# Two graph-attention layers in their factored form, with leaky slope, mask and softmax written out, in place of a merged weight and of maxima of exponentials

## The chip, the core and the metric

The kernel runs on one core of a Trainium2 chip. The metric is the device time of one execution in microseconds (us); the kernel before was run three times and took 3838.46 us in the median (3838.01 to 3841.55). One of these executions was profiled.

A core has a matrix engine (PE, TensorE), a vector engine (DVE, VectorE), an activation engine (ACT, ScalarE), a general engine (POOL, GpSimd) and a queue that issues transfers (SP). They run side by side, each in the order of its own instructions, and wait for each other by semaphores.

## What is computed

64 sequences of 256 positions and 256 features, all in fp32, pass through two blocks. The first block holds two graph-attention layers, then a residual sum with layernorm and a Relu feed-forward with layernorm. The second is a relational attention of 8 heads, then layernorm, a Gelu feed-forward and layernorm. The change touches only the graph-attention layers:

```python
def _gat(h, adj, W, a, out_features):
    Wh = jnp.matmul(h, W)
    Wh1 = jnp.matmul(Wh, a[:out_features])
    Wh2 = jnp.matmul(Wh, a[out_features:])
    e = Wh1 + jnp.swapaxes(Wh2, 1, 2)
    e = jax.nn.leaky_relu(e, negative_slope=ALPHA)
    scores = jnp.where(adj > 0, e, NEG)
    att = jax.nn.softmax(scores, axis=1)
    return jnp.matmul(att, Wh)

h = _gat(x, adj, W1, a1, Fout)
h = _gat(h, adj, W2, a2, W2.shape[1])
h = _layernorm(x + h, g_ln1, b_ln1)
```

The softmax runs over the rows (axis 1) of each sequence, so with the transposed adjacency `adjT`, which the host lays out, it runs along the free axis of a tile.

## The kernel before

Two sequences make a pair, and there are 32 pairs. A tile of a pair holds its 512 rows as four blocks of 128 partitions (index `k`; sequence `b` is `k // 2`). Products are 128x128 weights against up to 512 columns; each writes into one of 8 PSUM banks that all the work shares (`bank()`).

Each pair passes through four generators: `gat_layers`, `then_ff` (layernorm, Relu feed-forward, layernorm), `attention`, and `then_out` (projection by Wo, layernorm, Gelu feed-forward, layernorm, store). `together` steps two generators in turn, one `yield` each. The main loop runs `attention(pair)` with `then_ff(pair + 1)`, and then `then_out(pair)` with `gat_layers(pair + 2)`. Before the loop, `gat_layers(0)` runs alone and `gat_layers(1)` beside `then_ff(0)`; so 30 of the 32 graph-attention stages run beside a `then_out`. A scheduler then orders each engine's instructions, near the order in which the steps are written.

What the two graph layers do before the change:

- Setup (L113 to L121): W1 times [W2, W2 a2, a1] is multiplied once into `w12`, of 260 columns. Four columns of it give the scores of both layers.
- L376: `y = x w12`, 260 columns per block, copied out by ACT (L378). It contains the values of both layers' weights and the two scores of layer 1.
- `gat_weights` (L158 to L180): instead of exp(leaky(e1 + e2)) it uses the larger of two products of exponentials. ACT makes `up`, `low` and `ratio` of four columns each (L162 to L164), PE spreads `up` and `low` along rows by transposes of broadcast columns (L151), ACT copies one of the two (L168). DVE then makes `e` by a multiply and maximum (L174), and masks it with a maximum and a minimum against `adjT`, with the row sums beside it (L176). The reciprocal of the sums scales the values (L178, L180).
- L387: `e` times the scaled values, 258 columns, copied out by ACT (L389). Two of the columns are the scores of layer 2, so there is no second product with a weight.
- `gat_weights` again, then L398: `e` times values, and the residual sum (L220).

`steep` records the largest score for a range test at the end of the kernel (L158, L444). If a test fails, a general routine, which the change doesn't touch, computes everything anew; its code isn't shown here.

Other lines that are spoken of: L206 and L207 are the transposes of rows ahead of a feed-forward or of the attention, L232 and L235 its first product and activation, L245 its second product, L359 the projection by Wo, L189 to L198 layernorm, L193 its power on POOL, L215 the addition of a bias on POOL, L327 to L331 the division after the attention, L307 the mask of relation 1, L369 the largest value of `adjT`.

Of the kernel before, what the change touches and what calls it, by code (L numbers as in the profile page):

```python
# [10 lines left out]
F32 = mybir.dt.float32  # L11
I32 = mybir.dt.int32
U8 = mybir.dt.uint8
U32 = mybir.dt.uint32
AF = mybir.ActivationFunctionType
ALU = mybir.AluOpType
AX = mybir.AxisListType

P = 128
NEG = -9000000000000000.0  # L20
ALPHA = 0.2
EPS = 1e-5
SAFE = 1e25
STEEP = 30.0
SHIFT = 40.0
EVEN = 1e-37


@with_exitstack
def two_layers(ctx: ExitStack, tc: tile.TileContext, t: dict, out: bass.AP, flag: bass.AP):  # L30

# [5 lines left out]
    nc = tc.nc  # L40
    B, N, D = out.shape
    NPAIR = B // 2
    KC = D // P
# [9 lines left out]
    const = ctx.enter_context(tc.tile_pool(name="const", bufs=1))  # L53
# [12 lines left out]
    loaded = {0: load(0)}  # L66


    ident = const.tile([P, P], F32, name="ident")
    make_identity(nc, ident)  # L70
    shift = const.tile([P, 1], F32, name="shift")
    nc.vector.memset(shift, -SHIFT)
    mhalf = const.tile([P, 4], F32, name="mhalf")
    nc.vector.memset(mhalf, -0.5)
    ones = const.tile([P, DH], F32, name="ones")
    nc.vector.memset(ones, 1.0)
    reach = const.tile([P, NPAIR, 2 * KC], F32, name="reach")
    most = const.tile([P, NPAIR, 4], F32, name="most")
    steep = const.tile([P, NPAIR, 2], F32, name="steep")

    def weights(name, pool=const):
        w = t[name]
        kc, m = w.shape[0] // P, w.shape[1]
        s = pool.tile([P, kc, m], F32, name="w_" + name)
        nc.sync.dma_start(s, w.rearrange("(c p) m -> p c m", p=P))
        return s

    def on_all(name, n, pool=const):

        v = t[name]  # L90
        s = pool.tile([P, n], F32, name="b_" + name)
        nc.sync.dma_start(s, bass.AP(tensor=v.tensor, offset=v.offset, ap=[[0, P], [1, n]]))
        return s

    def column(name):
# [2 lines left out]
        nc.sync.dma_start(s, t[name])  # L98
        return s

    w12 = const.tile([P, KC, D + 4], F32, name="w12")
    with tc.tile_pool(name="setup", bufs=1) as setup, \
            tc.tile_pool(name="psetup", bufs=2, space=bass.MemoryType.PSUM) as psetup:
        w1T, a2 = weights("L0_gnn_W1T", setup), on_all("L0_gnn_a2", 2 * D, setup)
        right = setup.tile([P, KC, D + 4], F32, name="right")
        nc.sync.dma_start(right[:, :, :D], t["L0_gnn_W2"].rearrange("(c p) m -> p c m", p=P))
        nc.sync.dma_start(right[:, :, D + 2:], t["L0_gnn_a1c"])
        junk = setup.tile([P, D], F32, name="junk")  # L110
        for s in range(2):
            for c in range(KC):
                nc.vector.scalar_tensor_tensor(  # L113
                    junk, right[:, c, :D], 1.0, a2[:, s * D:(s + 1) * D], op0=ALU.mult, op1=ALU.mult,
                    accum_out=right[:, c, D + s:D + s + 1])
        for m in range(KC):
            pw = psetup.tile([P, 512], F32, name="pw")
            for c in range(KC):
                nc.tensor.matmul(pw[:, :D + 4], lhsT=w1T[:, c, m * P:(m + 1) * P], rhs=right[:, c],
                                 start=c == 0, stop=c == KC - 1)  # L120
            nc.vector.tensor_copy(w12[:, m], pw[:, :D + 4])  # L121
    ln = [tuple(on_all(n, D) for n in names) for names in (
        ("L0_gnn_g_ln1", "L0_gnn_b_ln1"), ("L0_gnn_g_ln2", "L0_gnn_b_ln2"),
        ("L1_gnn_g1", "L1_gnn_beta1"), ("L1_gnn_g2", "L1_gnn_beta2"))]
# [13 lines left out]
    work = ctx.enter_context(tc.tile_pool(name="work", bufs=1))  # L138
# [3 lines left out]
    def bank():  # L142
        return psum.tile([P, 512], F32, name="ps")

    def on_rows(col):

        p = bank()
        for k in range(4):  # L150
            nc.tensor.transpose(p[:, k * P:(k + 1) * P], col[:, k:k + 1].to_broadcast([P, P]), ident)  # L151
        return p

    def gat_weights(y, at, layer, pair, empty):

        nc.vector.tensor_reduce(steep[:, pair, layer:layer + 1], y[:, :, at:at + 2], axis=AX.XY, op=ALU.max,  # L158
                                apply_absolute_value=True)
        e1, e2 = y[:, :, at], y[:, :, at + 1]  # L160
        up, low, ratio = (small.tile([P, 4], F32, name=n) for n in ("up", "low", "ratio"))
        nc.scalar.activation(up, e1, AF.Exp, bias=shift[:, 0:1])  # L162
        nc.scalar.activation(low, e1, AF.Exp, bias=shift[:, 0:1], scale=ALPHA)
        nc.scalar.activation(ratio, e2, AF.Exp, scale=ALPHA - 1.0)  # L164
        yield
        p_up, p_low = on_rows(up), on_rows(low)
        rows_up = work.tile([P, 512], F32, name="rows_up")
        nc.scalar.activation(rows_up, p_up, AF.Copy)  # L168
        e = work.tile([P, 4, N], F32, name="e", bufs=2)
        adjT = loaded[pair][1]  # L170
        sums, rs = small.tile([P, 4], F32, name="sums"), small.tile([P, 4], F32, name="rs")
        for k in range(4):
            s = slice(k // 2 * N, k // 2 * N + N)
            nc.vector.scalar_tensor_tensor(e[:, k], p_low[:, s], ratio[:, k:k + 1], rows_up[:, s],  # L174
                                           op0=ALU.mult, op1=ALU.max)
            nc.vector.scalar_tensor_tensor(e[:, k], adjT[:, k], empty[:, k:k + 1], e[:, k],  # L176
                                           op0=ALU.max, op1=ALU.min, accum_out=sums[:, k:k + 1])
        nc.vector.reciprocal(rs, sums)  # L178
        for k in range(4):
            nc.vector.tensor_scalar(y[:, k, :at], y[:, k, :at], rs[:, k:k + 1], None, ALU.mult)  # L180
        yield
        return e

    def layernorm(r, gb):
        g, b = gb
# [180 lines left out]

    def gat_layers(pair):
        xT, adjT, x = loaded[pair]
        nc.vector.tensor_reduce(most[:, pair], adjT.bitcast(U32), axis=AX.X, op=ALU.max)  # L369
        empty = small.tile([P, 4], F32, name="empty")  # L370
        nc.vector.tensor_scalar(empty, most[:, pair], 0.0, EVEN, ALU.is_le, ALU.mult)
        y = work.tile([P, 4, D + 4], F32, name="xw", bufs=2)
        for k in range(4):
            ps = bank()
            for c in range(KC):
                nc.tensor.matmul(ps[:, :D + 4], lhsT=xT[:, c, k * P:(k + 1) * P], rhs=w12[:, c],  # L376
                                 start=c == 0, stop=c == KC - 1)
            nc.scalar.activation(y[:, k], ps[:, :D + 4], AF.Copy)  # L378
        yield
        e = yield from gat_weights(y, D + 2, 0, pair, empty)  # L380
        z = work.tile([P, 4, D + 2], F32, name="axw", bufs=2)
        for b in range(2):
            for i in range(2):
                ps = bank()
                for j in range(2):
                    k = 2 * b + j
                    nc.tensor.matmul(ps[:, :D + 2], lhsT=e[:, k, i * P:(i + 1) * P], rhs=y[:, k, :D + 2],  # L387
                                     start=j == 0, stop=j == 1)
                nc.scalar.activation(z[:, 2 * b + i], ps[:, :D + 2], AF.Copy)  # L389
        yield  # L390
        e = yield from gat_weights(z, D, 1, pair, empty)
        r = rows_tile()
        for b in range(2):
            ps = bank()
            for i in range(2):
                for j in range(2):
                    k = 2 * b + j
                    nc.tensor.matmul(ps[:, i * D:(i + 1) * D], lhsT=e[:, k, i * P:(i + 1) * P], rhs=z[:, k, :D],  # L398
                                     start=j == 0, stop=j == 1)
            add_rows(r, ps, x, b)  # L400
        rows[pair] = r
# [35 lines left out]
        del loaded[pair]  # L437


    ranges = ((reach, NPAIR * 4, N * SAFE), (most, NPAIR * 4, 1.0), (steep, NPAIR * 2, STEEP))  # L440
    count = const.tile([P, len(ranges)], F32, name="count")
    for n, (found, width, most_allowed) in enumerate(ranges):
        kept = const.tile([P, width], F32, name=f"kept{n}")
        nc.vector.tensor_scalar(kept, found.rearrange("p a b -> p (a b)"), most_allowed, None, ALU.is_le,  # L444
                                ALU.add, accum_out=count[:, n:n + 1])
    total = bank()
    nc.tensor.matmul(total[:1, :len(ranges)], lhsT=ones[:, :1], rhs=count, start=True, stop=True)
    all_of_them = const.tile([1, 1], F32, name="all_of_them")
    nc.vector.tensor_reduce(all_of_them, total[:1, :len(ranges)], axis=AX.X, op=ALU.add)
    nc.vector.tensor_scalar(flag, all_of_them, P * sum(w for _, w, _ in ranges) - 0.5, None, ALU.is_lt)  # L450


@with_exitstack
# [421 lines left out]
```

## Time and profile before

| what | value |
|---|---|
| median of three runs | 3838.46 us |
| the profiled execution | 3841.55 us |
| its span, from first to last instruction | 3839.8 us |
| mean granted clock of TensorE | 0.964 of full |
| ACT table loads (L235, L298), each | 63, 1.283 us |
| L376, x16 a pair, busy | 124.4 us |
| L151, x16 a pair, busy | 78.7 us |
| L387, x16 a pair, busy | 193.8 us |
| L398, x16 a pair, busy | 119.8 us |
| L174 and L176 on DVE, busy | 111.2 and 137.3 us |

Busy times are sums over the span of the time in which an engine worked on that group of instructions, overlaps counted once. An engine's row in the strip of 40 slices gives its busy tenths, and PEclk the clock that TensorE was granted, also in tenths. A weight load (PEld) runs ahead of, and beside, the products.

### The profile page before, as it was taken

The page shows a single profiled execution, that of the slowest core. Times are in us where ns is not written, and L with a number is a line of the kernel's source. Part 1 is how long each engine was busy: PE and PEld are TensorE (multiplying, and loading weights), DVE is VectorE, ACT ScalarE, POOL GpSimd, SP SyncE. Part 2 cuts the span into 40 slices and gives each one's busy share as a digit, 9 for nine tenths or more (in the row PEclk, how much of TensorE's full clock was granted, in tenths as well). Part 3 has the DMA queues.
Part 4 walks back from the last instruction along what each step waited for, and adds up shares of the span by engine and source line. Part 5 has one row for each costly group of instructions (what it writes and reads, how often), then busy time and mean ns, then how long its engine had stood idle before and what let it go on. Part 6 is the DMA issues. An engine that isn't in the chain of part 4 may idle for free. (4 is left out here: it accounts for less than half of the span.)

```text
span 3839.8 us, 46320 instructions
## 1 busy us (share of the span) xinstructions
PE 3530.9 (92%) x18698; PEld 2201.9 (57%) x18698; DVE 1967.2 (51%) x4825; ACT 1055.5 (27%) x1920; POOL 443.8 (12%) x518
## 2 busy tenths in 40 slices
PE   6999999999999999999999999999999999999998
PEld 4565565555655556556556565565565655656555
DVE  4454545545555455455454554555545545545444
ACT  1223223233222232222322323223233222232222
POOL 0111101101101011011110111110101101111010
PEclk9999999999999999999999999999999999999999
DMA  4000000000000000000000000000000000000000
GB/s 133 12 17 22 17 17 17 23 17 17 22 17 17 17 17 23 17 17 17 17 22 17 17 23 17 17 19 16 22 17 17 22 17 17 17 17 22 1 6 13
DMA packets 66862, 78.16 MB, mean 20 GB/s; under 512 B 3281, under 2 KB 57681, under 8 KB 66641
## 3 DMA queue, kind: packets, MB, share of 16 engines
q1 hardware_dynamic: 66640, 75.13, 6.2%
q8 instruction: 149, 2.44, 0.3%
q14 instruction: 73, 0.59, 0.0%
HBM read 58.34 MB, written 16.78 MB: 20 GB/s over the span
## 5 line engine op out<-in xcount | busy, mean ns | idle before, releaser
L232 PE MATMUL ps<-yT,w_L_gnn_w_ff 128*128 128x512 f32 x1024 | 473.2, 605 | 0.1
L245 PE MATMUL ps<-w_L_gnn_w_ff,ff 128*128 128x256 f32 x2048 | 467.1, 384 | 0.0
L232 PE MATMUL ps<-yT,w_L_gnn_W 128*128 128x512 f32 x1024 | 459.5, 597 | 1.0 <-ACT yT L207 1.0
L245 PE MATMUL ps<-w_L_gnn_W,ff 128*128 128x256 f32 x2048 | 447.2, 379 | 0.0
L245 PEld LDWEIGHTS ps<-w_L_gnn_w_ff,ff 128*128 128x128 f32 x2048 | 381.4, 190 | 83.9 <-issue 35.8
L245 PEld LDWEIGHTS ps<-w_L_gnn_W,ff 128*128 128x128 f32 x2048 | 389.1, 190 | 66.6 <-issue 15.3
L220 DVE TENSOR_TENSOR y<-ps,y 128x512 f32<-128x512 f32 x192 | 130.8, 681 | 536.7 <-PE ps L245 534.4
L307 DVE TENSOR_TENSOR m<-a,adjT 128x512 f32<-128x512 f32 x512 | 316.8, 686 | 147.2 <-ACT a L298 147.2
L327 DVE RECIPROCAL s<-ps 128x256 f32<-128x256 f32 x128 | 224.2, 1752 | 236.8 <-PE ps L321 236.8
L193 POOL TENSOR_TENSOR rstd<-rstd,mhalf 128x4 f32<-128x4 f32 x128 | 142.0, 1109 | 1732.2 <-DVE rstd L192 1732.2
L298 ACT ACTIVATE a<-ps 128x512 f32<-128x512 f32 x512 | 261.0, 614 | 215.7 <-PE ps L293 215.6
L232 PEld LDWEIGHTS ps<-yT,w_L_gnn_w_ff 128*128 128x128 f32 x1024 | 184.1, 189 | 233.2 <-issue 192.2
L232 PEld LDWEIGHTS ps<-yT,w_L_gnn_W 128*128 128x128 f32 x1024 | 193.8, 192 | 209.0 <-issue 195.7
L387 PE MATMUL ps<-xw,e 128*128 128x258 f32 x512 | 193.8, 559 | 129.9 <-DVE xw L180 129.9
L235 ACT ACTIVATE ff<-ps,c_L_gnn_b_ff 128x512 f32<-128x512 f32 x256 | 176.5, 690 | 373.2 <-PE ps L232 373.2
L235 ACT ACTIVATE ff<-ps,c_L_gnn_b 128x512 f32<-128x512 f32 x256 | 176.0, 687 | 369.6 <-PE ps L232 369.2
L378 ACT ACTIVATE xw<-ps 128x260 f32<-128x260 f32 x128 | 49.6, 387 | 769.0 <-PE ps L376 769.0
L387 PEld LDWEIGHTS ps<-xw,e 128*128 128x128 f32 x512 | 146.8, 294 | 172.1 <-DVE xw L180 138.1
L215 POOL TENSOR_TENSOR y<-y,b_L_gnn_bo 128x256 f32<-128x256 f32 x128 | 94.6, 770 | 1304.2 <-PE ps L206 1304.2
L174 DVE SCALAR_TENSOR_TENSOR e<-ps,ratio,rows_up 128x256 f32<-128x256 f32 x256 | 111.2, 474 | 236.2 <-ACT rows_up L168 235.2
L258 PE MATMUL ps<-wv,yTa 128*128 128x512 f32 x512 | 230.3, 592 | 0.0
L189 DVE BATCH_NORM_STATS2 st<-y 128x6 f32<-128x256 f32 x512 | 194.4, 412 | 5.4
(89 smaller groups left out, 4098.0 us busy)
## 6 DMA issues: line engine op xcount, KB each, us to landing
xT<-in_xT SPq DMA_DIRECT2D x32, 512.0 KB, 3.7
adjT<-in_adjT SPq DMA_DIRECT2D x32, 512.0 KB, 4.0
x<-in_x SPq DMA_DIRECT2D x32, 512.0 KB, 4.0
out<-y SPq DMA_DIRECT2D x32, 512.0 KB, 2.9
w_L_gnn_w_ff<-in_L_gnn_w_ff SPq DMA_DIRECT2D x2, 1024.0 KB, 10.4
w_L_gnn_W<-in_L_gnn_W SPq DMA_DIRECT2D x2, 1024.0 KB, 7.2
wv<-in_L_gnn_Wv SPq DMA_DIRECT2D x2, 256.0 KB, 7.2
w_L_gnn_W1T<-in_L_gnn_W1T SPq DMA_DIRECT2D x1, 256.0 KB, 6.8
```

The source lines that it names most:

```text
L174: nc.vector.scalar_tensor_tensor(e[:, k], p_low[:, s], ratio[:, k:k + 1], rows_up[:, s], op0=ALU.mult, op1=ALU.max)
L189: nc.vector.bn_stats(st[:, k, :], r[:, k, :])
L193: nc.gpsimd.tensor_tensor(rstd, rstd, mhalf, ALU.pow)
L220: nc.vector.tensor_tensor(r[:, s, :].rearrange("p k d -> p (k d)"), p, y[:, s, :].rearrange("p k d -> p (k d)"), ALU.add)
L232: nc.tensor.matmul(p1, lhsT=w1[:, c, m * P:(m + 1) * P], rhs=yT[:, c, :], start=c == 0, stop=c == KC - 1)
L235: nc.scalar.activation(h, p1, func, bias=b1[:, m:m + 1])
L245: nc.tensor.matmul(p2[:, j * D:(j + 1) * D], lhsT=f[m][:, k * P:(k + 1) * P], rhs=w2[:, m, :], start=m == 0, stop=m == NF - 1)
L258: nc.tensor.matmul(ps, lhsT=yT[:, c, at:at + P], rhs=wv[:, c].rearrange("p r m -> p (r m)"), start=c == 0, stop=c == KC - 1)
L298: nc.scalar.activation(a, ps[o], AF.Exp)
L307: nc.vector.tensor_tensor(m, a, adj, ALU.mult)
L327: nc.vector.reciprocal(s, po[:, N:])
L387: nc.tensor.matmul(ps[:, :D + 2], lhsT=e[:, k, i * P:(i + 1) * P], rhs=y[:, k, :D + 2], start=j == 0, stop=j == 1)
```

## The change

The merged weight, the exponentials of the scores and the transposes go. Each layer now does what the reference writes. `p1` is the first score of all columns, spread on all partitions by a weight whose columns are all the same (`wide`); `p2` is the second score, one column per block. ACT adds them, DVE applies the leaky slope, writes NEG where `adjT` isn't positive and takes the row maximum, ACT takes Exp with row sums. The values are a product of their own, scaled by the reciprocal of the sums while they are copied from PSUM. Layer 1 writes its result transposed (`hT`), as layer 2 takes it. `masked` is made once per pair. The range test on `steep` goes. The products of the heads with the relations' values, in the second block, are the same in both kernels.

```diff
-    w12 = const.tile([P, KC, D + 4], F32, name="w12")
...
+    def gat_weights(w_name, a_name, setup):
+
+        w = weights(w_name)
+        a = on_all(a_name, 2 * D, setup)
+        wa = const.tile([P, 2, KC, 1], F32, name="wa_" + w_name)
+        junk = setup.tile([P, D], F32, name="junk")
+        for s in range(2):
+            for c in range(KC):
+                nc.vector.scalar_tensor_tensor(
+                    junk, w[:, c, :], 1.0, a[:, s * D:(s + 1) * D], op0=ALU.mult, op1=ALU.mult,
+                    accum_out=wa[:, s, c, :])
+        wide = const.tile([P, KC, P], F32, name="wide_" + w_name)
+        for c in range(KC):
+            nc.vector.tensor_copy(wide[:, c, :], wa[:, 0, c, :].to_broadcast([P, P]))
+        return w, wide, wa[:, 1]
...
-    def on_rows(col):
...
-    def gat_weights(y, at, layer, pair, empty):
...
+    def gat_attention(aT, gw, masked):
+
+        w, wide, wa2 = gw
+        p1 = bank()
+        for c in range(KC):
+            nc.tensor.matmul(p1, lhsT=wide[:, c, :], rhs=aT[:, c, :], start=c == 0, stop=c == KC - 1)
+        p2 = bank()
+        for k in range(4):
+            for c in range(KC):
+                nc.tensor.matmul(p2[:, k:k + 1], lhsT=aT[:, c, k * P:(k + 1) * P], rhs=wa2[:, c, :],
+                                 start=c == 0, stop=c == KC - 1)
+        wh2 = small.tile([P, 4], F32, name="wh2")
+        nc.vector.tensor_copy(wh2, p2[:, :4])
+        e = work.tile([P, 4, N], F32, name="e")
+        for k in range(4):
+            b = k // 2
+            nc.scalar.activation(e[:, k, :], p1[:, b * N:(b + 1) * N], AF.Identity, bias=wh2[:, k:k + 1])
+        yield
+        ef = e.rearrange("p k n -> p (k n)")
+        nc.vector.scalar_tensor_tensor(ef, ef, ALPHA, ef, op0=ALU.mult, op1=ALU.max)
+        nc.vector.copy_predicated(ef, masked, neg.to_broadcast([P, 4 * N]))
+        nm = small.tile([P, 4], F32, name="nm")
+        nc.vector.tensor_reduce(nm, e, axis=AX.X, op=ALU.max, negate=True)
+        sums = small.tile([P, 4], F32, name="sums")
+        for k in range(4):
+            nc.scalar.activation(e[:, k, :], e[:, k, :], AF.Exp, bias=nm[:, k:k + 1], accum_out=sums[:, k:k + 1])
+        yield
+        rs = small.tile([P, 4], F32, name="rs")
         nc.vector.reciprocal(rs, sums)
-        for k in range(4):
-            nc.vector.tensor_scalar(y[:, k, :at], y[:, k, :at], rs[:, k:k + 1], None, ALU.mult)
-        yield
-        return e
+        wh = work.tile([P, 4, D], F32, name="wh")
+        for b in range(2):
+            pw = bank()
+            for j in range(2):
+                k = 2 * b + j
+                for c in range(KC):
+                    nc.tensor.matmul(pw[:, j * D:(j + 1) * D], lhsT=aT[:, c, k * P:(k + 1) * P], rhs=w[:, c, :],
+                                     start=c == 0, stop=c == KC - 1)
+            for j in range(2):
+                k = 2 * b + j
+                nc.vector.tensor_scalar(wh[:, k, :], pw[:, j * D:(j + 1) * D], rs[:, k:k + 1], None, ALU.mult)
+        yield
+        return e, wh
...
     def gat_layers(pair):
         xT, adjT, x = loaded[pair]
+        masked = work.tile([P, 4 * N], U8, name="masked")
+        nc.vector.tensor_scalar(masked, adjT.rearrange("p k n -> p (k n)"), 0.0, None, ALU.is_le)
         nc.vector.tensor_reduce(most[:, pair], adjT.bitcast(U32), axis=AX.X, op=ALU.max)
...
+        e, wh = yield from gat_attention(xT, gat1, masked)
+        hT = work.tile([P, KC, 512], F32, name="hT")
+        for c in range(KC):
             ps = bank()
+            for b in range(2):
+                for j in range(2):
+                    k = 2 * b + j
+                    nc.tensor.matmul(ps[:, b * N:(b + 1) * N], lhsT=wh[:, k, c * P:(c + 1) * P], rhs=e[:, k, :],
+                                     start=j == 0, stop=j == 1)
+            nc.scalar.activation(hT[:, c, :], ps, AF.Copy)
+        yield
+        e, wh = yield from gat_attention(hT, gat2, masked)
         r = rows_tile()
         for b in range(2):
             ps = bank()
             for i in range(2):
                 for j in range(2):
                     k = 2 * b + j
-                    nc.tensor.matmul(ps[:, i * D:(i + 1) * D], lhsT=e[:, k, i * P:(i + 1) * P], rhs=z[:, k, :D],
+                    nc.tensor.matmul(ps[:, i * D:(i + 1) * D], lhsT=e[:, k, i * P:(i + 1) * P], rhs=wh[:, k, :],
                                      start=j == 0, stop=j == 1)
             add_rows(r, ps, x, b)
         rows[pair] = r
```

More of the change, by code (lines that the diff above doesn't have):

```diff
@@ L23 @@
 SAFE = 1e25
-STEEP = 30.0
-SHIFT = 40.0
-EVEN = 1e-37
 @with_exitstack
@@ L70, in two_layers @@
     make_identity(nc, ident)
-    shift = const.tile([P, 1], F32, name="shift")
-    nc.vector.memset(shift, -SHIFT)
+    neg = const.tile([P, 1], F32, name="neg")
+    nc.vector.memset(neg, NEG)
     mhalf = const.tile([P, 4], F32, name="mhalf")
@@ L78, in two_layers, with weights @@
     most = const.tile([P, NPAIR, 4], F32, name="most")
-    steep = const.tile([P, NPAIR, 2], F32, name="steep")
-    def weights(name, pool=const):
+    def weights(name):
         w = t[name]
         kc, m = w.shape[0] // P, w.shape[1]
-        s = pool.tile([P, kc, m], F32, name="w_" + name)
+        s = const.tile([P, kc, m], F32, name="w_" + name)
         nc.sync.dma_start(s, w.rearrange("(c p) m -> p c m", p=P))
@@ L99, in column @@
         return s
-    w12 = const.tile([P, KC, D + 4], F32, name="w12")
[L104 to L109, printed above, removed]
+    def gat_weights(w_name, a_name, setup):
+        w = weights(w_name)
+        a = on_all(a_name, 2 * D, setup)
+        wa = const.tile([P, 2, KC, 1], F32, name="wa_" + w_name)
         junk = setup.tile([P, D], F32, name="junk")
@@ L113, in two_layers @@
                 nc.vector.scalar_tensor_tensor(
[L114 to L121, printed above, removed]
+                    junk, w[:, c, :], 1.0, a[:, s * D:(s + 1) * D], op0=ALU.mult, op1=ALU.mult,
[4 more added lines that the diff above has]
+        return w, wide, wa[:, 1]
+    with tc.tile_pool(name="setup", bufs=1) as setup:
+        gat1 = gat_weights("L0_gnn_W1", "L0_gnn_a1", setup)
+        gat2 = gat_weights("L0_gnn_W2", "L0_gnn_a2", setup)
     ln = [tuple(on_all(n, D) for n in names) for names in (
@@ L143, in bank @@
         return psum.tile([P, 512], F32, name="ps")
-    def on_rows(col):
-        p = bank()
-        for k in range(4):
-            nc.tensor.transpose(p[:, k * P:(k + 1) * P], col[:, k:k + 1].to_broadcast([P, P]), ident)
-        return p
-    def gat_weights(y, at, layer, pair, empty):
[L158 to L164, printed above, removed]
-        yield
[L166 to L171, printed above, removed]
-        for k in range(4):
[L173 to L177, printed above, removed]
-        nc.vector.reciprocal(rs, sums)
-        for k in range(4):
-            nc.vector.tensor_scalar(y[:, k, :at], y[:, k, :at], rs[:, k:k + 1], None, ALU.mult)
@@ L368, in gat_layers @@
         xT, adjT, x = loaded[pair]
+        masked = work.tile([P, 4 * N], U8, name="masked")
+        nc.vector.tensor_scalar(masked, adjT.rearrange("p k n -> p (k n)"), 0.0, None, ALU.is_le)
         nc.vector.tensor_reduce(most[:, pair], adjT.bitcast(U32), axis=AX.X, op=ALU.max)
[L370 to L373, printed above, removed]
+        e, wh = yield from gat_attention(xT, gat1, masked)
+        hT = work.tile([P, KC, 512], F32, name="hT")
+        for c in range(KC):
             ps = bank()
[L375 to L378, printed above, removed]
-        yield
[L380 to L384, printed above, removed]
+            for b in range(2):
                 for j in range(2):
                     k = 2 * b + j
-                    nc.tensor.matmul(ps[:, :D + 2], lhsT=e[:, k, i * P:(i + 1) * P], rhs=y[:, k, :D + 2],
+                    nc.tensor.matmul(ps[:, b * N:(b + 1) * N], lhsT=wh[:, k, c * P:(c + 1) * P], rhs=e[:, k, :],
                                      start=j == 0, stop=j == 1)
-                nc.scalar.activation(z[:, 2 * b + i], ps[:, :D + 2], AF.Copy)
+            nc.scalar.activation(hT[:, c, :], ps, AF.Copy)
         yield
-        e = yield from gat_weights(z, D, 1, pair, empty)
+        e, wh = yield from gat_attention(hT, gat2, masked)
         r = rows_tile()
@@ L437, in two_layers @@
         del loaded[pair]
[L440 to L444, printed above, removed]
+    count = const.tile([P, 2], F32, name="count")
+    for n, (values_of, most_allowed) in enumerate(((reach, N * SAFE), (most, 1.0))):
+        kept = const.tile([P, NPAIR * 4], F32, name=f"kept{n}")
+        nc.vector.tensor_scalar(kept, values_of.rearrange("p a b -> p (a b)"), most_allowed, None, ALU.is_le,
                                 ALU.add, accum_out=count[:, n:n + 1])
     total = bank()
[L447 to L450, printed above, removed]
+    nc.tensor.matmul(total[:1, :2], lhsT=ones[:, :1], rhs=count, start=True, stop=True)
+    both = const.tile([1, 1], F32, name="both")
+    nc.vector.tensor_reduce(both, total[:1, :2], axis=AX.X, op=ALU.add)
+    nc.vector.tensor_scalar(flag, both, 2 * P * NPAIR * 4 - 0.5, None, ALU.is_lt)
 @with_exitstack
@@ L859 @@
     laid["xT"] = np.ascontiguousarray(x.reshape(B // 2, 2, N, D).transpose(0, 3, 1, 2))
-    laid["L0_gnn_W1T"] = np.ascontiguousarray(laid["L0_gnn_W1"].T)
-    laid["L0_gnn_a1c"] = np.ascontiguousarray(laid["L0_gnn_a1"].reshape(2, -1, P).transpose(2, 1, 0))
     laid["adjT"] = np.ascontiguousarray(adj.transpose(0, 2, 1))
```

## Prediction

> **What bounds the kernel now.** I read the page's busy times first, then the strips in 40 slices, the waits of TensorE, the groups by shape, and last the timeline of one period.
>
> ```profile
> span 3839.8 us, 46320 instructions
> PE 3530.9 (92%) x18698; PEld 2201.9 (57%) x18698; DVE 1967.2 (51%) x4825; ACT 1055.5 (27%) x1920; POOL 443.8 (12%) x518
> PE   6999999999999999999999999999999999999998
> PEclk9999999999999999999999999999999999999999
> ```
>
> TensorE is busy 92% from end to end and no other engine passes 51%. What is left is 309 us of idle PE and whatever the clock strip hides, which is below full in every slice. The waits say where:
>
> ```profile
> PE ps L387 <- DVE xw L180: 129.9, 32, 4.2
> PE ps L206 <- DVE y L198: 54.0, 65, 4.2
> PE ps L398 <- DVE axw L180: 34.1, 32, 4.3
> PE ps L359 <- DVE oT L331: 31.5, 32, 3.1
> PE ps L151 <- ACT up L162: 26.0, 32, 0.9
> ```
>
> Columns: total us, times, longest. Nearly all of it lies once per pair of sequences, around the first graph layer. The timeline of TensorE there (start, length, group, idle before it):
>
> ```profile
> 1817.25 2.42 PE L359 MATMUL ps<-w_L_gnn_Wo,oT 128*128 128x256 f32 x10
> 1819.51 2.36 PE L376 MATMUL ps<-w,xT 128*128 128x260 f32 x10
> 1822.77 1.56 PE L359 MATMUL ps<-w_L_gnn_Wo,oT 128*128 128x256 f32 x6 [0.90 <-DVE oT L331]
> 1824.17 1.48 PE L376 MATMUL ps<-w,xT 128*128 128x260 f32 x6
> 1826.46 0.65 PE L151 MATMUL ps<-ident,up 128*128 128x128 f32 x4 [0.81 <-ACT up L162]
> 1826.95 0.60 PE L151 MATMUL ps<-ident,low 128*128 128x128 f32 x4
> 1828.45 1.14 PE L206 MATMUL ps<-ident,y 128*128 128x128 f32 x6 [0.91 <-DVE y L198]
> 1830.02 0.44 PE L206 MATMUL ps<-ident,y 128*128 128x128 f32 x2 [0.43 <-DVE y L198]
> 1834.64 6.28 PE L387 MATMUL ps<-xw,e 128*128 128x258 f32 x16 [4.19 <-DVE xw L180]
> ```
>
> The reader should see two things. From the Wo product to the product with e, PE idles 7.2 us. And the 16 instructions that end the row take 6.28 us, where the same shape (L376, x10 from 1819.51 to 1821.87) runs at 0.226 us each, 3.6 us in all: the clock has dropped. Their weight loads have a median of 337 ns against 190 at L376. Over all 32, L387 is busy 193.8 us, so (193.8 - 32 x 3.55) / 32 = 2.5 us of slow clock per pair. The period, from this L359 to the one two pairs on (2054.70), is 118.7 us a pair.
>
> [...] a 4.19 us gap, then about 6 us slow. [...] the mask step L176 took 0.85 and 0.93 us beside GpSimd's bias adds and 0.47 without.
>
> **The change, part by part.** An fp32 product is two PE instructions, a transpose one. PE rates from the timeline: 0.43 us per instruction of 512 columns (16 from 1722.27 to 1729.13), 0.22 of 256, 0.11 per transpose.
> Removed per pair: L376 16 x 0.226 = 3.6; the 16 transposes of L151 1.76; L387 at full clock 3.5. Sum 8.9 us.
> Added: the row score p1, 4 instructions of 512 a layer, 2 x 1.74 = 3.5; the column score p2, 16 instructions of one column a layer; wh, 16 of 256 a layer, 2 x 3.5 = 7.0; hT, 16 of 256, 3.5. The last product stays. The trace has no one-column product with full weights. [...] from above, a load that hides under nothing, 0.19 (the LDWEIGHTS rows), and what the three-column product L447 lasts beyond its own load, 0.17 - 0.08: 0.28. I take 0.12 since loads run ahead of products here: 2 x 1.92 = 3.8. Sum 17.8 us. PE gains 8.9 us of work a pair, 285 us in all, if all of it were on the path.
>
> Not all is: the first layer lies in the stretch with 7.2 us idle. I lay out both stretches, with time 0 at the first Wo product, in the order in which the changed code puts each engine's instructions.
>
> *Stretch A, to the end of the first product with e.* Before: 17.39 to the start of L387, 3.5 of work, 2.5 slow: 23.4. After, PE: ten Wo instructions to 2.26, p1 to 4.0, p2 to 5.9, two of wh, then the other six Wo (oT is ready at 5.5, so the 0.90 wait goes), to 7.7, the rest of wh to 10.8. Then PE waits for VectorE. VectorE is in order: it is done with oT at 5.46, waits for p2 and copies wh2 (6.3); layernorm of the first half (two bn_stats 0.75, aggregates 0.30, two L195 0.86) to 8.1, residual add 0.63, leaky 1.2 (ScalarE has made e in 4 x 0.3 by 7.6), bn_stats and one aggregate 0.87, copy_predicated, two L195, aggregate and rstd 1.1, row maximum 1.22 (the row of L369, 1024 elements), four L198 2.1. Leaky over 1024 is scaled from L307 (512 in 0.62): 1.2. copy_predicated isn't in the trace; from below one pass of 1024 (1.1), from above two (2.3); I take 1.2. The sum puts the last L198 at 16.4. ScalarE's four Exp, about 0.4 each from L378, start after the maximum at 14.3 and end beside L198. rs 0.2; the first scaled wh at 16.7. Then hT, 3.5 of work. PE was idle from 10.8 to about 14.6 and had only eight transposes until 16.7, so I let it pay the same 2.5 slow: end at 22.7. **Stretch A: -0.7 us.**
>
> *Stretch B, from there to the second feed-forward product.* Before 19.26 (1722.27 to 1741.53): L232 13.8, L151 0.88, L398 3.53, a wait of 0.96. After: L232 13.8, p1 1.74, p2 1.92, wh 3.5, the last product 3.53: 24.5. Do waits hide in it? ScalarE must do two more table loads a pair (Gelu, Exp, Gelu; 1.28 each in this trace). Counted from hT's end: e 7.4 to 9.0 after p2; maximum at 12.6; table load and Exp after the fifth Gelu, 13.1 to 16.2; wh scaled by 17.9; the last product is due at 21. That leaves 3 us, so the slower ScalarE costs nothing unless the chain slips by that; then each us beyond it is 30 us. Banks: the sixth Gelu frees its bank at 18.2, before the rotation needs it. **Stretch B: +5.2 us.**
>
> The rest of the period, 76 us, is untouched: most stays, and masked (1.2 us on VectorE) stands where VectorE waits for Exp. Loads of xT are released a few us later but are needed a whole stage later, and a load of 512 KB lands in 4 us.
>
> *Ends.* Pair 0 runs alone. The merged weight's setup on PE (12.04 to 16.4) goes, but each layer now has leaky, mask, maximum, Exp and wh in a row; I add them up to about 49 us against 46.2 at the end of its last product: +3. Pair 1 beside a Relu feed-forward: 8.9 of work less about 2 of waits: +7.
>
> Sum: 30 pairs x (5.2 - 0.7) = 135, +10: +145. The profiled execution took 3841.55 us (its span 3839.8): 3986. It is the slowest of three, 3.1 over their median, so the median goes to 3984.
>
> **Rivals.** *The clock stays up.* If the transposes and the scattered work before hT count as busy, the 2.5 us a pair go: -75, 3909. [...] Against: 6 us pass with hardly any products.
> *VectorE's chain is longer.* copy_predicated in two passes (+1.1) and GpSimd's adds beside the late L198 and the wh scaling (+1.2): hT starts 2.3 later in each pair, +69: 4053.
> *One-column products are dear.* At 0.28 they cost 16 x 0.16 more in B and as much in A, where VectorE waits for them: +5.1 a pair, 4137.
> *Faster.* The mechanism is that the new PE work fills the wait of stretch A. A without waits and slow clock is 3.5 + 1.74 + 1.92 + 3.5 + 0.9 + 3.5 = 15.1, or -8.3, which beats +5.2 by 3.1: 30 x -3.1 + 10 = -83, 3758. It decides once hT can start, warm, before 14.7 rather than 16.7. Against it: 10 us of VectorE work stand between p2 and wh.
> That the general path is taken can be set aside: the range tests on adj and the sums stay, and adj holds 0 and 1.
>
> **Numbers.** Forecast 0.55, clock stays up 0.17, longer chain 0.15, dear small products 0.08, faster 0.03, no change 0.02. Under 0.2% this kernel's measurement can't be told from no change. The range 3905 to 4065 covers the first three cases and the lower part of the fourth. Faster 0.03, same 0.02, slower 0.95.
>
> **What would show it.** p2 at about 0.12 us per instruction; PE waiting near 4 us for y and almost nothing for wh in layer 2; hT's products slow in most pairs; period near 123.2; table loads doubled with no wait behind them. It is wrong if p2 takes over 0.2, if PE waits at the last product or at the feed-forward for ScalarE, or if stretch A is below 18 us.

## The result and the profile after

The changed kernel takes 3983.48 us in the median of four runs (3977.33 to 3985.10), against 3839.15 for the kernel before, run beside it: a ratio of 1.0372, with a 95% interval of 1.0354 to 1.0390. That is 144.3 us more; the forecast was 145 more.

From the page of the changed kernel: the span, the busy times of the engines, and the strips of TensorE and of its clock.

```profile
span 3981.2 us, 48796 instructions
...
PE 3795.5 (95%) x19970; PEld 2424.9 (61%) x19970; DVE 2004.0 (50%) x4257; ACT 1230.3 (31%) x2300; POOL 442.4 (11%) x518
...
PE   7999999999999999999999999999999999999998
...
PEclk8999999999999999999999999999999999999999
```

PE is busy 265 us longer than before, but the span of the profiled execution grew by only 141: the rest of the added work stands where PE used to wait. Its idle time fell from 309 to 186 us. The waits of TensorE after the change (total us, times, longest):

```profile
PE ps L205 <- DVE y L197: 122.2, 48, 4.2
PE ps L378 <- DVE wh L179: 11.4, 22, 1.0
...
PE ps L378 <- ACT yT L206: 8.6, 8, 1.3
...
PE ps L389 <- DVE wh L179: 6.2, 1, 6.2
PE ps L358 <- DVE oT L330: 4.1, 2, 3.1
```

The waits for xw (129.9), for oT (31.5), for up (26.0) and for axw in layer 2 (34.1) have gone or shrunk to single cases. One has grown: the transposes ahead of the second feed-forward (L205, which was L206) wait 122 us for the layernorm in front of them. The timeline of TensorE over one pair's graph layers shows both stretches of the prediction (start, length, group, idle before it):

```profile
1894.41 2.43 PE L358 MATMUL ps<-w_L_gnn_Wo,oT 128*128 128x256 f32 x10
1896.67 1.88 PE L145 MATMUL ps<-xT,wide_L_gnn_W 128*128 128x512 f32 x4
1898.39 1.84 PE L149 MATMUL ps<-wa_L_gnn_W,xT 128*128 128x1 f32 x16
1900.09 0.68 PE L175 MATMUL ps<-w_L_gnn_W,xT 128*128 128x256 f32 x2
1900.61 1.46 PE L358 MATMUL ps<-w_L_gnn_Wo,oT 128*128 128x256 f32 x6
1901.90 3.19 PE L175 MATMUL ps<-w_L_gnn_W,xT 128*128 128x256 f32 x14
1908.47 1.53 PE L205 MATMUL ps<-ident,y 128*128 128x128 f32 x8 [3.38 <-DVE y L197]
1911.05 6.54 PE L378 MATMUL ps<-e,wh 128*128 128x256 f32 x16 [1.05 <-ACT yT L206]
1917.43 3.60 PE L231 MATMUL ps<-yT,w_L_gnn_W 128*128 128x512 f32 x8
1920.86 1.88 PE L145 MATMUL ps<-hT,wide_L_gnn_W 128*128 128x512 f32 x4
1922.58 1.84 PE L149 MATMUL ps<-wa_L_gnn_W,hT 128*128 128x1 f32 x16
1924.28 7.11 PE L231 MATMUL ps<-yT,w_L_gnn_W 128*128 128x512 f32 x16
1931.23 3.62 PE L175 MATMUL ps<-w_L_gnn_W,hT 128*128 128x256 f32 x16
1934.69 3.60 PE L231 MATMUL ps<-yT,w_L_gnn_W 128*128 128x512 f32 x8
1938.12 3.62 PE L389 MATMUL ps<-wh,e 128*128 128x256 f32 x16
1941.57 13.98 PE L244 MATMUL ps<-w_L_gnn_W,ff 128*128 128x256 f32 x64
```

Stretch A runs from 1894.41 to 1917.43. p1, p2 and wh stand where PE waited for oT, up and xw before; a wait of 3.38 us and one of 1.05 are left, and the 16 instructions of L378 still take over 6 us. Stretch B, from 1917.43 to 1941.57, has no wait at all. Means over the 30 pairs that run beside a `then_out`, read off this view for every pair:

| per pair, us | before | after | forecast |
|---|---|---|---|
| first Wo product to first product with e | 17.40 | 16.65 | 16.7 |
| the 16 instructions of that product | 5.95 | 6.10 | 6.0 |
| stretch A | 23.35 | 22.75 | 22.7 |
| stretch B | 19.26 | 24.14 | 24.5 |
| period | 118.33 | 122.61 | 123.2 |

30 x 4.28 is 128.3. The first Wo product of all comes at 176.31 us in place of 160.78, which is another 15.5; and from the end of the 30 periods to the last instruction the changed kernel takes 126.7 us in place of 129.1. Together that is the 141.4 between the two profiled executions.

### The profile page after: what moved, and what is told of

It is laid out like the page before. It is cut to its first block, busy times and chain, and to the rows that moved or that the text cites. A ratio compares the mean times of both kernels' runs of the same rounds, so it can differ in the third digit from the quotient of the medians.

```text
span 3981.2 us, 48796 instructions
## 1 busy us (share of the span) xinstructions
PE 3795.5 (95%) x19970; PEld 2424.9 (61%) x19970; DVE 2004.0 (50%) x4257; ACT 1230.3 (31%) x2300; POOL 442.4 (11%) x518
## 5 line engine op out<-in xcount | busy, mean ns | idle before, releaser
L156 ACT ACTIVATE e<-ps,wh 128x256 f32<-128x256 f32 x256 | 100.2, 474 | 825.8 <-DVE wh L152 815.0
L205 PE MATMUL ps<-ident,y 128*128 128x128 f32 x768 | 126.6, 300 | 122.2 <-DVE y L197 122.2
L378 PE MATMUL ps<-e,wh 128*128 128x256 f32 x512 | 198.0, 571 | 22.9 <-DVE wh L179 11.4
L152 DVE COPY wh<-ps 128x4 f32<-128x4 f32 x64 | 10.4, 162 | 398.8 <-PE ps L149 398.8
L206 ACT ACTIVATE yTa<-ps 128x512 f32<-128x512 f32 x64 | 34.7, 595 | 549.2 <-PE ps L205 549.2
```

Of the source, the lines that this page charges most:

```text
L156: nc.scalar.activation(e[:, k, :], p1[:, b * N:(b + 1) * N], AF.Identity, bias=wh2[:, k:k + 1])
L205: nc.tensor.transpose(pt[:, k * P:(k + 1) * P], y[:, k, c * P:(c + 1) * P], ident)
L378: nc.tensor.matmul(ps[:, b * N:(b + 1) * N], lhsT=wh[:, k, c * P:(c + 1) * P], rhs=e[:, k, :], start=j == 0, stop=j == 1)
```

## The experiments

A sum that comes out right can have two wrong terms. So the experiments took the terms one by one: which engine ends each stretch, what ScalarE costs, why the product with e is slow, and whether the wait of stretch A is what made the change cheap.

### The same cut, and the same addition, in each of the two layers

If stretch A is set by VectorE's chain and stretch B by PE's work, one edit must act in opposite ways in the two layers. Two kernels shorten PE's work, in layer 1 or in layer 2 (`blocks` is 1 in that layer and 4 in the other):

```diff
-        for k in range(4):
+        blocks = 1 if gw is gat1 else 4
+        for k in range(blocks):
             for c in range(KC):
                 nc.tensor.matmul(p2[:, k:k + 1], lhsT=aT[:, c, k * P:(k + 1) * P], rhs=wa2[:, c, :],
...
-            nc.scalar.activation(e[:, k, :], p1[:, b * N:(b + 1) * N], AF.Identity, bias=wh2[:, k:k + 1])
+            nc.scalar.activation(e[:, k, :], p1[:, b * N:(b + 1) * N], AF.Identity,
+                                 bias=wh2[:, k % blocks:k % blocks + 1])
```

> The changed kernel, with layer 1's column score p2 computed for one block of rows in place of four (its 16 one-column instructions a pair become 4; the other blocks use the first block's score, so three quarters of this score are left out). 12 x 0.106 = 1.28 us of PE work a pair less. Theory (stretch A ends when VectorE's chain does, and VectorE waits only 0.40 us for p2): at most 0.4 us a pair, so 12 us less than the changed kernel's 3983, about 3971, and PE's wait at L205 grows by about 0.9 us. Rival (PE is 95% busy, so each us of its work counts wherever it stands): 32 x 1.28 = 41 us less, 3942.

> The same cut in layer 2 alone (three quarters of layer 2's column score are left out). Theory (stretch B is PE work without waits): 32 x 1.28 = 41 us less, about 3942. Rival (stretch B is held by ScalarE's chain of table loads, Exp and Gelu, or by VectorE's mask chain): less than half of it, 3965 to 3983.

Two others lengthen VectorE's chain in one layer (`gat2` for the second of them):

```diff
         nc.vector.copy_predicated(ef, masked, neg.to_broadcast([P, 4 * N]))
+        if gw is gat1:
+            nc.vector.copy_predicated(ef, masked, neg.to_broadcast([P, 4 * N]))
```

> The changed kernel, with layer 1's copy_predicated issued twice (the second writes the same values). 1.3 us of VectorE a pair more. Theory (VectorE's chain sets stretch A): 30 x 1.3 = +39, about 4022, and PE's wait ahead of the transposes in L205 1.2 us longer. Rival (PE's work sets stretch A and VectorE has slack): no change, 3983.

> The same doubling in layer 2 alone. Theory (stretch B is PE work; wh is scaled 2.4 us before the last product is due, and 1.3 us later the row maximum is still early enough): no change, 3983 within 8. Rival (the chain mask, maximum, Exp, wh is what ends the wait in layer 2 as well): +39, 4022.

Measured, beside the changed kernel's 3983.5 (means per pair, read off the timeline as in the table above):

| run | median us | to product with e | its length | stretch B |
|---|---|---|---|---|
| changed kernel | 3983.5 | 16.65 | 6.10 | 24.14 |
| p2 cut in layer 1 | 3950.5 | 16.09 | 5.71 | 24.14 |
| p2 cut in layer 2 | 3936.1 | 16.65 | 5.92 | 22.80 |
| mask twice in layer 1 | 4017.7 | 18.28 | 5.62 | 24.14 |
| mask twice in layer 2 | 3982.2 | 16.65 | 6.06 | 24.14 |

In layer 2 a microsecond of PE is a microsecond (B falls by 1.34 for 12 instructions of 0.106; the 47 us of this run hold 0.18 more a pair, by which the slow product of layer 1 got shorter) and 1.3 us more of VectorE are nothing. In layer 1, VectorE's time is paid in full: the start of the product moves by 1.63, although the run is only 34 us longer, since the product behind it got 0.48 shorter. The 1.63 is more than the 1.23 between the starts of the doubled instruction and of the next one. VectorE's timeline of this kernel shows the rest:

```profile
1922.21 1.34 DVE L162 COPY_PREDICATED_SCALAR e<-masked,neg 128x1024 f32 x1
1923.44 0.47 DVE L199 SCALAR_TENSOR_TENSOR y<-y,rstd,b_L_gnn_beta 128x256 f32<-128x256 f32 x1
1923.83 1.21 DVE L164 TENSOR_REDUCE nm<-e 128x4 f32<-128x1024 f32 x1
1924.96 1.39 DVE L199 SCALAR_TENSOR_TENSOR y<-y,rstd,b_L_gnn_beta 128x256 f32<-128x256 f32 x3
```

One step of layernorm now stands ahead of the row maximum, 0.39 us from start to start: 1.23 + 0.39 = 1.62.

The cut in layer 1 missed its expectation: 33 us less, where the theory gave at most 12 and the rival 41. Less than half of the 1.28 us went into the start of the product (0.56; the copy of p2 now comes as soon as VectorE is through with oT). So the PE work of p2 is itself a link of VectorE's chain, as far as VectorE waits for it. Another 0.39 is that the product itself ran slow for a shorter time. This was not foreseen, and comes back below. The two make 28 us; the first Wo product of all comes 5.4 us earlier.

### ScalarE's table loads

```diff
-        r = yield from feed_forward(r, ff1, AF.Gelu)
+        r = yield from feed_forward(r, ff1, AF.Relu)
```

> The changed kernel with Relu in place of Gelu in the second feed-forward (so Gelu is left out and the output differs): all ACT table loads after the first go, 4 a pair of 1.283 us, and ScalarE never switches between Exp and Gelu in stretch B. Theory (ScalarE is off the path in both stretches): no change, 3983 within 8. Rival (the two added loads a pair are paid): 30 x 2.57 = 77 less, 3906, or at least a few tens.

3982.96 us, 0.5 below the changed kernel. One table load of 1.283 us remains in the whole trace, in place of 124 (62, 31, 30 and 1 at four lines). In the changed kernel the groups by shape list them so (busy us, mean ns, idle before):

```profile
L234 ACT ACT_TABLE_LOAD x62 | 79.5, 1283 | 1.1
...
L297 ACT ACT_TABLE_LOAD x31 | 39.8, 1283 | 0.5
L165 ACT ACT_TABLE_LOAD x30 | 38.5, 1283 | 0.5
```

Together 158 us of ScalarE, and none of it on the path: stretch B stays at 24.14.

### Keeping TensorE's clock up

```diff
             for j in range(2):
                 k = 2 * b + j
                 nc.vector.tensor_scalar(wh[:, k, :], pw[:, j * D:(j + 1) * D], rs[:, k:k + 1], None, ALU.mult)
+        if gw is gat1:
+            spare = bank()
+            for n in range(4):
+                nc.tensor.matmul(spare, lhsT=wide[:, 0, :], rhs=aT[:, 0, :], start=n == 0, stop=n == 3)
         yield
```

> The changed kernel with four products of 512 columns into a spare bank, which nobody reads, placed by the order of PE's instructions between the rest of wh and the transposes of L205, in the wait of 3.4 us. Theory (the 16 instructions of hT run slow because PE idled before them): 3.4 us of added work cost nothing, hT takes 3.5 to 4 us in place of 6.1, 30 x 2.2 to 2.6 less, 3905 to 3917. Rival (hT's products are slow by themselves, for their operands or their waits): hT stays at 6.1 and the time at 3983 or above.

```diff
         e = yield from gat_weights(y, D + 2, 0, pair, empty)
+        spare = bank()
+        for n in range(4):
+            nc.tensor.matmul(spare, lhsT=w12[:, 0, :P], rhs=xT[:, 0, :], start=n == 0, stop=n == 3)
         z = work.tile([P, 4, D + 2], F32, name="axw", bufs=2)
```

> The kernel before with the same four products, one of which stands between the transposes of L206 and three ahead of L387. Theory: L387's 16 instructions fall from 5.95 to about 3.6 us and little else changes, 30 x 2.3 = 70 less, about 3768, below both kernels. Rival (slow by themselves, or the filler delays L387): 3838 or more.

The changed kernel with the spare products takes 3903.5 us, 80 less; the kernel before with them 3771.8, a ratio of 0.9823 (0.9807 to 0.9839). The changed kernel's timeline with the spare products (L183):

```profile
1862.21 3.19 PE L175 MATMUL ps<-w_L_gnn_W,xT 128*128 128x256 f32 x14
1865.23 3.60 PE L183 MATMUL ps<-xT,wide_L_gnn_W 128*128 128x512 f32 x8
1868.78 1.53 PE L209 MATMUL ps<-ident,y 128*128 128x128 f32 x8
1871.36 3.69 PE L382 MATMUL ps<-e,wh 128*128 128x256 f32 x16 [1.05 <-DVE wh L179]
```

PE does 3.5 us more, its product with e starts at the same time after Wo (16.65 in the mean, within a hundredth), and takes 3.53 us in the mean of 30 pairs, in place of 6.10. So the slow clock costs 2.57 us a pair in the changed kernel, and 5.95 - 3.55 = 2.40 in the one before. It is the stretch ahead of it, in which PE had little to do, that does this, not the product.

### Taking the wait of stretch A away

The kernel before was then staged so that the graph layers of the next pair start inside the attention stage, where PE has work. First three of their six steps were moved, then all six, and the changed kernel was staged likewise with all seven:

```diff
-        together(attention(pair), part(then_ff, pair + 1))
-        together(then_out(pair), part(gat_layers, pair + 2))
+        graph = part(gat_layers, pair + 2)
+        together(attention(pair), part(then_ff, pair + 1), chain(repeat(None, 3), islice(graph, 6)))
+        together(then_out(pair), graph)
```

The two numbers are 5 and 3 for the first run, 3 and 6 for the second, 2 and 7 for the changed kernel; `together` takes any number of generators.

> The kernel before with useful work in place of the filler: the first three steps of the next pair's graph layers are issued inside the attention stage, so that the exponentials and masks of layer 1 are made while PE has attention work, and L387 stands beside the Wo product. Theory (the waits of stretch A are VectorE's chain standing behind Wo): most of the 7.2 us of waits and the slow clock go, 118.3 a pair falls to 110 to 114, 3580 to 3720. Rival (the wait for the layernorm of the Wo product takes their place, with its own slow clock): 3780 to 3838.

> The kernel before with all six steps of the next pair's graph layers issued in the attention stage (three steps after its start); only the last product, L398, stands behind Wo. before_mid53 moved one layer and the wait went over to L398; now both layers' chains on VectorE have attention work of PE beside them. Theory: of the 7.2 us of waits of stretch A and the 0.96 of L398 only the layernorm of the Wo product is left, about 4 us, and with it the slow clock; 118.3 a pair becomes 113 to 115, 3680 to 3740. Rival (VectorE becomes the bound of the attention stage and gives the gain back there): above 3780.

> The changed kernel staged in the same way (all seven steps of its graph layers in the attention stage, two steps after its start). Its net PE work is 8.5 us a pair: p1 3.5, p2 3.4, wh 7.0, hT 3.5, less L376 3.6, L151 1.8, L387 3.5. Theory (as it stands, the changed kernel pays only 4.3 a pair, since stretch A had a wait that its work fills): with no such wait the difference to the kernel before in the same staging is the full work, 30 x 8.5 = 255 plus about 15 for pairs 0 and 1, some 270 in place of 144. Rival (the change costs what it costs, 4 to 5 us a pair, wherever it is staged): the difference stays at 130 to 160.

| kernel | median us | ratio to before (95%) | period |
|---|---|---|---|
| before, three steps early | 3790.2 | 0.9872 (0.9856 to 0.9889) | 116.74 |
| before, all steps early | 3770.4 | 0.9822 (0.9805 to 0.9838) | 116.16 |
| changed, all steps early | 3991.0 | 1.0395 (1.0377 to 1.0412) | 122.95 |

Neither of the two stagings of the kernel before reached what the theory gave, and the waits of TensorE say why. With three steps early:

```profile
PE ps L398 <- DVE axw L180: 129.0, 32, 4.3
PE ps L206 <- DVE y L198: 53.2, 65, 4.2
PE ps L359 <- DVE oT L331: 31.6, 32, 3.1
```

The wait of 129.9 us for layer 1 has become one of 129.0 for layer 2: the next chain of VectorE stands in the same place behind Wo. With all steps early:

```profile
PE ps L206 <- DVE y L198: 141.9, 37, 4.2
PE ps L387 <- DVE xw L180: 51.5, 32, 4.2
PE ps L359 <- DVE oT L331: 27.4, 32, 3.1
```

Both graph chains are gone from that place, and the layernorm of the Wo product has it: 4.23 us a pair at L206. A second wait, 1.57 a pair, has come up at L387, inside the attention stage.

Between the two kernels in this staging lie 220.5 us, where the theory said 270 and its rival 130 to 160. The theory's amount is right for PE's work, but it took both kernels to be free of waits. By the periods they differ by 6.79: 8.5 of work, less the 1.57 at L387, which the changed kernel doesn't have, and 0.33 less at the layernorm leave 6.6. With 20 us more before the first Wo product (189.19 against 168.95) and 29 such periods, 29 x 6.79 + 20 = 217, and the two profiled executions lie 217.5 apart. So the change costs 6.8 us a pair where its work meets little waiting, and 4.3 where a wait takes up half of it.

### Where the spare products have to stand

Both runs of this section start from the kernel before with all steps early.

```diff
         r = projected(attended.pop(pair), rows.pop(pair))
         yield
+        spare = bank()
+        for n in range(4):
+            nc.tensor.matmul(spare, lhsT=wo[:, 0, :P], rhs=wv[:, 0].rearrange("p r m -> p (r m)"),
+                             start=n == 0, stop=n == 3)
```

> The same with four products of 512 columns, which nobody reads, between L398 and the transposes of L206. Theory: the rest of the slow clock goes too, 2.0 to 2.5 us a pair, 60 to 75 below the run without them. Rival (the layernorm's wait is shorter than the filler, 3.4 us, or did not slow the clock): equal or slower than that run.

3768.95 us, within 2 of the run without: the expectation failed. PE's wait at L206 fell from 4.23 to 1.23 us a pair, for 3.45 us of spare work, and L232 behind it stayed slow in 18 of the 30 pairs. Two neighbouring pairs:

```profile
1926.73 15.45 PE L232 MATMUL ps<-yT,w_L_gnn_W 128*128 128x512 f32 x32 [0.58 <-ACT yT L207]
2043.31 14.00 PE L232 MATMUL ps<-yT,w_L_gnn_W 128*128 128x512 f32 x32 [0.58 <-ACT yT L207]
```

In the 18 pairs the granted clock was at a half for 3.41 us, and L232 got nearly all of it; without spare products it was at a half for 6.83 us in every pair, but L232 met only part of that (15.03 us in the mean). The mean granted clocks of the two profiled executions, 0.987 and 0.968, fit: they make about 98 and 241 us at a half in all, 143 apart, and 30 x 6.83 - 18 x 3.41 is 143.5. The last run kept three spare products ahead of the transposes and put others between them:

```diff
+            if k < 3:
+                nc.tensor.matmul(spare[:, :256], lhsT=y[:, k, :P], rhs=y[:, k, :256], start=k == 0, stop=k == 2)
```

> before_all_early_filler with the spare products placed otherwise: three of 512 columns ahead of the transposes of the second feed-forward and one of 256 columns after each of the first three pairs of them. With all of them ahead, PE's wait went (141.9 us to 48.6) but L232 still ran slow for 1.6 us a pair (15.3 to 15.5 against 13.8). Theory [...]: with products between them the slow clock goes, 1.6 us a pair less and up to 0.7 more for the products in the way, 27 to 48 less than 3769, 3720 to 3742. Rival (the slow clock has another reason, or the products delay L232 by what they save): 3765 or more.

3752.74 us, a ratio of 0.9776 (0.9760 to 0.9789): faster than both kernels and the fastest of the study, though less of a gain than expected. Its timeline:

```profile
1909.76 2.74 PE L429 MATMUL ps<-wv,w_L_gnn_Wo 128*128 128x512 f32 x6
1914.15 0.41 PE L207 MATMUL ps<-ident,y 128*128 128x128 f32 x2 [1.65 <-DVE y L198]
1914.40 0.60 PE L209 MATMUL ps<-y 128*128 128x256 f32 x2
1914.83 0.38 PE L207 MATMUL ps<-ident,y 128*128 128x128 f32 x2
1915.05 0.60 PE L209 MATMUL ps<-y 128*128 128x256 f32 x2
1915.48 0.38 PE L207 MATMUL ps<-ident,y 128*128 128x128 f32 x2
1915.70 0.60 PE L209 MATMUL ps<-y 128*128 128x256 f32 x2
1916.14 0.38 PE L207 MATMUL ps<-ident,y 128*128 128x128 f32 x2
1917.10 14.00 PE L245 MATMUL ps<-yT,w_L_gnn_W 128*128 128x512 f32 x32 [0.58 <-ACT yT L211]
```

The 32 instructions of the next product take 14.00 us, now in all 30 pairs. Over the whole trace that group is busy 450.0 us in place of 482.0, 1.0 a pair. The 1.6 that was expected had been read from slow pairs alone; the products in the way took 0.37 back (2.95 from the first transpose to L245, 2.58 before).

## Why the prediction was right

*What bounds the kernel.* The split into a stretch set by VectorE's chain and one set by PE's work is shown. The doubled mask costs 34 us in layer 1 and nothing in layer 2. The cut of p2 is less clean: it counts in full in layer 2, and with 0.56 of its 1.28 us in layer 1, where VectorE waits for p2.

*Stretch B.* Forecast +5.2, measured +4.88. The one-column product takes 0.106 us an instruction (16 in 1.70, from 1922.58 to 1924.28), not 0.12; the transposes of the kernel before start 0.109 us apart where they stand back to back. The rival in which these products are dear is out. wh was scaled by 1935.8 and the product due at 1938.1, so 2.4 us of slack where 3 were counted.

*Stretch A.* Forecast -0.7, measured -0.60, with the product's start off by 0.05. Here terms did cancel. copy_predicated held VectorE for 1.21 us from start to start here (1.2 taken, between bounds of 1.1 and 2.3 for one pass and two; the four instructions of L180 pass 1032 columns in 1.15 us in the kernel before), so the rival with two passes is out. Exp is followed by an instruction that reads its sums, so four take 2.1 us from first to last, not 1.6. The late L198 (L197 now) took 1.66 in some pairs and 2.13 in others, where 2.1 was taken; GpSimd's bias adds begin 1.1 us after it, as in the kernel before. The chain also ended in another place: VectorE waited for Exp before the reciprocal, 0.62 us behind a short L197 and 0.15 behind a long one, so maximum, Exp and scaling closed it, not the layernorm beside them.

*Slow clock.* 2.5 forecast, 2.57 measured by the spare products. The rival in which the clock stays up fell: the gap shrank to 3.4 us, and the product was slow in all 30 pairs. That the mean stayed at 2.5 was luck in part: single pairs lie between 1.1 and 2.9, for a reason that the forecast did not have (see the last section).

*ScalarE.* Costed at nothing for two more table loads a pair, and shown to be nothing.

*Ends.* The term that was mis-sized: +10 forecast, +15.5 measured ahead of the first Wo product and -2.4 behind the last period, which the forecast left out. Pair 0 ended its last product at 51.66 in place of 46.24 (+5.4, not +3). Pair 1 then took 54.9 to the end of its feed-forward product in place of 44.8 (+10, not +7): it waited 2.67 us for its first transposes, and PE's clock over 46 to 92 us was 0.89 where it was 1.00 before.

The sum, 128.3 + 15.5 - 2.4, is the 141.4 between the profiled executions. The medians lie 144.3 apart, because the profiled execution of the kernel before is the slowest of its four. The forecast had 7 us too much in the periods (135) and 3 too little at the ends, so that 145 meets 144.3 within 1 us is luck; its terms are good to some 7 us. Its period before, 118.7, came from two pairs; the mean of 30 is 118.33.

## What to carry to other kernels

A busy share of 95% doesn't say that each microsecond of that engine's work counts: cut the same work in two places, and see which cut the time follows. Added work is cheap where the engine waited, and the price comes due once someone removes that wait (4.3 us a pair here, 6.8 after restaging). A wait that is moved away gives its place to the next chain behind the same instruction, so list all the chains that end there before promising the whole wait.

## What had not been expected

The length of the slow product goes with the period of the whole loop. In us, the first 12 pairs in order, from the timelines of four kernels:

```
before         period 118.33   6.6 5.2 6.1 6.6 5.2 6.1 6.6 5.2 5.9 6.5 5.1 6.1
p2_l2_short    period 121.09   5.4 6.5 5.4 6.5 5.3 6.5 5.4 6.6 5.4 6.6 5.4 6.6
mask_l1_twice  period 123.76   6.2 5.5 5.1 5.0 6.4 5.6 5.2 5.0 6.5 5.7 5.2 5.0
after          period 122.61   5.3 5.8 6.1 6.2 6.2 6.3 6.3 6.3 6.4 6.4 6.4 6.4
```

In the records of the granted clock that the traces of the kernel before and of the changed kernel hold, the clock is either full or a half, and all its changes (71 and 73) fall on one grid with a step of 3.413 us, to 0.0003 of a step. In such steps the four periods are 34.67, 35.48, 36.26 and 35.92 long, and the rows repeat after three, two and four pairs, and drift slowly in the last. So where the grid falls on the loop is a term that no count of work shows. The slow part differs between 2.1 and 2.6 us a pair among these kernels, up to 14 us in all. The gap ahead of the product differs among them too, and no run changed the period alone, so how much of this is the period's isn't shown; nor is it that the 0.39 us which the cut in layer 1 won beside its work come from there.

The other is what counts as idle. The last two runs can be read as if transposes were idle time: L232 was slow in 18 pairs with only transposes ahead of it, and in none with products between them. The clock of the kernel before says otherwise. From the start times of PE's instructions in the two traces, the steps of the grid at full clock between 200 and 3600 us, by what PE starts in the step (us at 0.109 a transpose):

| PE starts in a step | steps, clock half in the next | steps, clock full in the next |
|---|---|---|
| before: transposes alone, at most 10 (1.09 us) | 28 | 0 |
| before: transposes alone, 12 to 14 (1.31 to 1.53 us) | 0 | 10 |
| before: products, with or without transposes | 0 | 893 |
| after: transposes alone, at most 8 (0.87 us) | 27 | 0 |
| after: products, with or without transposes | 0 | 915 |

So transposes alone kept the clock up where 12 or more started in a step, and did not where 10 or fewer did; eight of them, as ahead of L232, are 0.87 us. Whether products have the same border isn't shown, as no step with products holds less than 1.7 us of work. What the products between them added was work: six instructions of 256 columns, which start 0.216 us apart in the kernel before, are 1.3 us, and the mean granted clock went from 0.987 to 0.996. The busy time of the profile hides this, for transposes that come in singly are recorded as longer than 0.109 us each (two of them with 0.38 us in the last timeline above): one step of the kernel before, 406.20 to 409.61, shows 2.20 us busy for 14 transposes, an estimated 1.5 us of work at 0.109 each, and the clock is full after it.
